# A graph-attention and low-rank expert kernel: the neighbours' sum as two float32r products of a split operand

## The chip, the cores and the metric

The kernel runs on one core of a Trainium2 chip. The metric is the device time of one execution in microseconds (us). The engines are named as in the profile: PE is TensorE (PEld its weight loads), DVE is VectorE, ACT is ScalarE, POOL is GpSimd and SP is SyncE, which here only issues transfers.

## The reference, cut to what matters

There are 128 images (batch entries) of 128 rows and 1024 columns, 16 heads of 64 columns, and 8 experts of rank 16.

```python
h  = layernorm(x)                              # x: (128, 128, 1024)
Wh = h @ W                                     # W: (1024, 1024), 16 heads of 64
e  = leaky_relu(Wh1 + Wh2, 0.2)                # one score per row and head
att = softmax(where(adj == 0, -9e15, e)) * adj # adj: 0/1, (128, 128, 128)
x  = x + elu(att @ Wh)
y  = layernorm(x)
gates = softmax(top2(y[:, 0, :] @ router_w.T)) # 2 of 8 experts for each image
x  = x + y + low-rank sum of the two chosen experts (y @ down, then @ up)
```

The score `e` depends on the row alone, not on the neighbour. So `att @ Wh` is one number per row and head times a plain sum of the neighbours' `Wh` with the 0/1 matrix `adj`. That product, "the neighbours' sum", is what the change rewrites.

## The kernel before, in words

**Tiling.** The images are handled in 64 pairs; `q` counts the pairs, images `2q` and `2q+1` are t = 0 and t = 1 of pair `q`. Two pairs make a group of four images, and the gates and experts are worked group by group (32 groups).

**Projection.** `project(q)` multiplies a pair by `W` with seven block products instead of eight (a Strassen-Winograd scheme on 2 x 2 blocks, the two images being one block dimension): `product_1`, `product_6`, `product_2`, `product_5`, `product_7`, `product_3`, `product_4`, in this order; below they are P1 to P7. Each is 8 matmuls of 260 columns in fp32 (L287). Their left operands are the transposed images `xt` and sums of them, which POOL makes in `pair_sums` (tiles `s1`, `s2`, `s4` and one in place). Results leave PSUM through ACT copies (L312, L316) and DVE additions (L299) into `u` tiles and the pair's tile `wh`. `wh[:, t, h]` has 512 columns of `Wh` and 8 score columns for image t and half h. `W` is centred over its rows beforehand, so `wh` lacks only the row scale 1/deviation, `rstd`, of the first layer norm.

**Attention.** `attention_weights(q)` first has ACT multiply the pair's two `adj_f` tiles by `rstd` (L361), since the neighbour's row scale belongs to the contracted index; then DVE makes the softmax factor `att` in small operations with one exponential on ACT (L371) between. `attend(i)` is the neighbours' sum of image i: two fp32 matmuls, one for each half, with `adj_f` as the stationary and `wh` as the moving operand (L389). `update(i)` multiplies by `att` (L399) and adds the ELU to `x` (L406 on ACT, L407 and L408 on DVE).

**Experts.** `second_stats` gives the second layer norm's scales. `turn(i)` transposes the updated image with a DMA (ACT copies to `halves`, L439, DMA to `tt`), and `rejoin` puts it into `y_t` (ACT, L445). `join` adds `y` to `x` in place (ACT, L461). For a group, `logits` makes the router's product (PE, L469), `choose` and `weigh` the two gates (DVE, with one exponential `pr` on ACT, L497), `fetch` spreads the choice over the partitions (PE `pb` L518, DVE `at_down` L520) and gathers the experts' rows with nine indirect DMAs on POOL's queue (`down` L532, `up` L536). `ffn_down` (PE `pd` L546, ACT `dn` L552) and `ffn_up` (PE `pu` L562, DVE L566) finish the group, and SP writes the result.

**Order of work.** All engine queues are in program order, written out by hand. In step q, eight lists of work `gaps[0]` to `gaps[7]` stand between the seven products: what is in `gaps[k]` is issued ahead of the (k+1)th product. `attention_weights(q-1)` is in gap 0, the two `attend` of pair q-1 in gaps 1 and 2. In odd steps `fetch` is at the head of gap 1, `ffn_down` of gap 4, and `ffn_up` in gaps 5 and 6. In even steps `logits`, `choose`, `weigh` are in gap 6, with `group_adj` and `load_adj` of another group behind them. So on PE an odd pair runs P1, `pb`, attend, P6, attend, P2, P5, `pd`, P7, `pu`, P3, `pu`, P4; an even one P1, attend, P6, attend, P2, P5, P7, P3, logits, P4.

**Buffers.** PSUM holds two tiles `pw` of two banks for the products and four one-bank tiles `pm` for all else. `xt`, `wh`, `hp`, `adj_f`, `tt`, `s1`, `s2`, `s4` have two buffers each, `x` ten.

Of the kernel before, what the change touches and what calls it, by code (L numbers as in the profile page):

```python
# [7 lines left out]

F32 = mybir.dt.float32
I32 = mybir.dt.int32  # L10
U32 = mybir.dt.uint32
U16 = mybir.dt.uint16
AF = mybir.ActivationFunctionType
ALU = mybir.AluOpType
# [9 lines left out]
def adj_ffn_kernel(  # L24
# [13 lines left out]
    nc = tc.nc  # L38
    B, N, D = x.shape
    P = 128  # L40
    KC = D // P
    KH = KC // 2
# [7 lines left out]
    HALF = 512  # L50
    NH = D // HALF
    HPH = HALF // F
    CPH = HALF // P
    NG, _, G, _ = adj.shape
    HE = HALF + HPH
# [3 lines left out]
    const = ctx.enter_context(tc.tile_pool(name="const", bufs=1))  # L59
    work = ctx.enter_context(tc.tile_pool(name="work", bufs=2))  # L60
# [6 lines left out]
        mybir.EngineType.PE, mybir.EngineType.DVE, mybir.EngineType.Activation,  # L67
        mybir.EngineType.Pool, mybir.EngineType.SP}))

    X, XT, MV, RSTD, WH, PH, SUMS, ATT, TT = ({} for _ in range(9))  # L70
    GRP = {}


# [6 lines left out]
    w_sb = const.tile([P, 7, KH, HE], F32, name="w_sb")  # L80
    BLOCK = [[B11, B21], [T1, B22]]

    def load_pair(q):
        XT[q] = work.tile([P, 2, KC, P], F32, tag="xt", name="xt")
        for t in range(2):
            nc.sync.dma_start(XT[q][:, t], x_t[2 * q + t])
        for i in (2 * q, 2 * q + 1):
            X[i] = work.tile([P, D], F32, tag="x", name="xn", bufs=10)
            nc.sync.dma_start(X[i], x[i])

    def load_adj(g):
        adj_i = work.tile([P, G, N], I32, tag="adj_i", name="adj_i", bufs=1)
        nc.sync.dma_start(adj_i, adj[g])
        adj_f = work.tile([P, G, N], F32, tag="adj_f", name="adj_f")
        nc.gpsimd.dma_start(adj_f, adj_t[g])
        GRP[g] = {"adj_i": adj_i, "adj_f": adj_f}

# [1 line left out]

        return w_sb[:, BLOCK[h][k // KH], k % KH]  # L100

    a_rows = work.tile([1, 2, D], F32, tag="wh", name="a_rows")
    nc.sync.dma_start(a_rows, a[None])
    for h in range(NH):
        for k in range(KC):
            (nc.scalar, nc.sync)[k % 2].dma_start(
                w_at(h, k)[:, 0:HALF], w[k * P:(k + 1) * P, h * HALF:(h + 1) * HALF])
    load_pair(0)
    router_sb = const.tile([P, KC, E], F32, name="router_sb")
    down_sb = work.tile([P, G * TOP, R, KC], F32, tag="down", name="down_sb", bufs=1)  # L110
    load_adj(0)
# [6 lines left out]
    nc.vector.memset(half_pow, -0.5)  # L118
    one_row = const.tile([1, P], F32, name="one_row")
    nc.vector.memset(one_row, 1.0)  # L120
    mean_of = const.tile([P, P], F32, name="mean_of")
    nc.vector.memset(mean_of, 1.0 / D)
    ones_g = const.tile([G, P], F32, name="ones_g")
    nc.vector.memset(ones_g, 1.0)
# [117 lines left out]
    def pair_sums(q):  # L242

        xt = XT[q]
        a11, a12 = xt[:, 0, 0:KH], xt[:, 0, KH:KC]
        a21, a22 = xt[:, 1, 0:KH], xt[:, 1, KH:KC]
        s1, s2, s4 = (work.tile([P, KH, P], F32, tag=n, name=n) for n in ("s1", "s2", "s4"))
        nc.gpsimd.tensor_tensor(s1, a21, a22, ALU.add)
        nc.gpsimd.tensor_tensor(s2, s1, a11, ALU.subtract)  # L249
        nc.gpsimd.tensor_tensor(a21, a11, a21, ALU.subtract)  # L250
        nc.gpsimd.tensor_tensor(s4, a12, s2, ALU.subtract)
        SUMS[q] = (s1, s2, a21, s4)

    def group_adj(g):

# [14 lines left out]
    def project(q):  # L270

        xt = XT.pop(q)
        a11, a12, a22 = xt[:, 0, 0:KH], xt[:, 0, KH:KC], xt[:, 1, KH:KC]
        s1, s2, s3, s4 = SUMS.pop(q)

        wh = WH[q] = work.tile([P, 2, NH, HE], F32, tag="wh", name="wh")

        def bank():
            return ps_w.tile([P, 2, HALF], F32, tag="pw", name="pw")

        def product(dst, first, lhs, rhs):
            for j in range(2):
                for k in range(KH):
                    nc.tensor.matmul(dst[:, j, 0:QE], lhs[:, k, :],  # L287
                                     w_sb[:, rhs, k, j * QE:(j + 1) * QE],
                                     start=(first and k == 0), stop=(k == KH - 1),
                                     skip_group_check=not first)  # L290

        def cols(t):
            return t.rearrange("p (j c) -> p j c", j=2)

        def temp(tag):
            return work.tile([P, HE], F32, tag=tag, name=tag, bufs=1)

        def read(dst, src, plus):
            nc.vector.tensor_tensor(cols(dst), src[:, :, 0:QE], cols(plus), ALU.add)  # L299

        p1, u2, u4 = (temp(n) for n in ("p1", "u2", "u4"))
        banks = {}

        def to(name):
            if name not in banks:
                banks[name] = bank()
                return banks[name], True
            return banks[name], False

        def product_1():  # L310
            product(*to("x"), a11, B11)
            nc.scalar.copy(cols(p1), banks["x"][:, :, 0:QE])  # L312

        def product_2():
            product(*to("x"), a12, B21)
            nc.scalar.copy(cols(wh[:, 0, 0]), banks["x"][:, :, 0:QE])  # L316

        def product_6():
            product(*to("y"), s2, T2)
            read(u2, banks["y"], p1)  # L320

        def product_5():
            product(*to("y"), s1, T1)
            read(u4, banks["y"], p1)
            if q == 0:
                read(wh[:, 1, 1], banks["z"], u4)

        def product_7():
            product(*to("z"), s3, T3)
            if q:  # L330
                read(wh[:, 1, 1], banks["z"], u4)

        def product_3():
            product(*to("y"), s4, B22)
            read(wh[:, 0, 1], banks["y"], p1)

        def product_4():
            product(*to("z"), a22, NT4)
            read(wh[:, 1, 0], banks["z"], u2)


        for step in ((product_1, product_6, product_2, product_5, product_7, product_3, product_4)
                     if q else
                     (product_1, product_2, product_6, product_7, product_5, product_3, product_4)):
            step()
            yield

    def attention_weights(q):

        g, first = divmod(2 * q, G)
        st = GRP[g]
# [2 lines left out]
        n1, n0, neg = (st[n][:, pair, None].to_broadcast(shape) for n in ("n1", "n0", "neg"))  # L356
        raw = WH[q].rearrange("p t h c -> p (t h) c")[:, :, HALF:HE]
        rstd = RSTD[q]
        for t in range(2):
            cols = st["adj_f"][:, first + t]  # L360
            nc.scalar.mul(cols, cols, rstd[:, t:t + 1])  # L361
        e = small.tile(shape, F32, tag="e", name="e")
        nc.vector.scalar_tensor_tensor(e.rearrange("p t (h c) -> p (t h) c", h=NH), raw, ALPHA,
                                       raw, op0=ALU.mult, op1=ALU.max)
# [4 lines left out]
        nc.vector.tensor_tensor(p[:, 0], e, m, ALU.subtract)  # L369
        nc.vector.tensor_tensor(p[:, 1], neg, m, ALU.subtract)  # L370
        nc.scalar.activation(p, p, AF.Exp)  # L371
        z = small.tile([P, 2, 2, H], F32, tag="z", name="z")
        nc.vector.tensor_mul(z[:, 0], p[:, 0], n1)
        nc.vector.tensor_mul(z[:, 1], p[:, 1], n0)
# [8 lines left out]
    def attend(i):  # L383

        g, t = divmod(i, G)
        wh = WH[i // 2][:, i % 2]
        PH[i] = [ps_m.tile([P, HALF], F32, tag="pm", name="ph") for _ in range(NH)]
        for h in range(NH):
            nc.tensor.matmul(PH[i][h], GRP[g]["adj_f"][:, t, :], wh[:, h, 0:HALF],  # L389
                             start=True, stop=True)  # L390

    def update(i):

# [190 lines left out]
    def prepare(gaps):  # L584

        prod = {}
        gaps[0] += [
            (spread_a,), (column_means, 0), (column_means, 1),
            (lambda: prod.update({1: score_products(1)}),),
            (score_columns_at_once, 0), (score_means, 0), (center_block, 0, B11),  # L590
            (pair_sums, 0), (weights_3_main,)]
        gaps[1] += [(center_block, 0, B21)]
        gaps[2] += [(lambda: score_columns(1, prod[1]),), (weights_3_scores,),
                    (combine, T2, T3, B11, ALU.add), (score_means, 1), (center_block, 1, T1)]
        gaps[3] += [(combine, T1, T1, B11, ALU.subtract)]
        gaps[4] += [(center_block, 1, B22)]
        gaps[5] += [(combine, NT4, B21, T2, ALU.subtract)]
        gaps[6] += [(first_stats, 0), (first_stats, 1)]

    NQ = B // 2  # L600


    for q in range(NQ + 2):
        gaps = [[] for _ in range(8)]
        if q == 0:
            prepare(gaps)
        g, part = divmod(q - 2, 2)
        ffn = 0 <= g < NG
        if ffn and not part:
# [15 lines left out]
            gaps[5] += [(join, i), (join, i + 1)]  # L625
        if q + 1 < NQ:
            gaps[3].append((first_stats, 2 * q + 2))
            gaps[4].append((pair_sums, q + 1))
            gaps[5].append((first_stats, 2 * q + 3))
        if ffn and part:  # L630
            gaps[1].insert(0, (fetch, g))
            gaps[4].insert(0, (ffn_down, g))
            gaps[5].insert(0, (ffn_up, (g, 0)))
            gaps[6].append((ffn_up, (g, 1)))
        if q % 2 == 0 and q < NQ:
            gaps[6].append((group_adj, q // 2))
            if q // 2 + 1 < NG:
                gaps[6].append((load_adj, q // 2 + 1))

        if q + 1 < NQ:  # L640
            load_pair(q + 1)
        if q == 1:
            slot, down_row, up_row = experts()
        products = project(q) if q < NQ else iter(())
# [41 lines left out]
```

## Time and profile before

| What | Value |
|---|---|
| Median of 3 runs | 2066.79 us (2066.38 to 2068.28) |
| The profiled execution's own time | 2068.33 us |
| Its span, first to last instruction | 2066.6 us |
| PE busy | 2022.0 us |
| DVE busy | 1526.5 us |
| ACT busy | 982.1 us |
| POOL busy | 835.3 us |
| Neighbours' sum on PE (L389), 512 records | 243.7 us busy |
| Mean granted TensorE clock | 0.987 |

All of it is one execution. A fp32 matmul appears as two records with a weight load each, so the 256 products of L389 are 512 records. Their busy times overlap a little; the time that a matmul adds is read from the distance of starts, or from the chain of work that ended last. In a timeline, the columns are the start, the duration in us, the engine, the line and operation, output and input, and in brackets the idle time of the engine ahead of it with what ended it. A bracket on an engine with nothing due later costs nothing.

### The profile page before, as it was taken

The numbers are of one execution on the slowest core, as the hardware profiler recorded it, in microseconds if no ns is written. First come the engines' busy times: TensorE is split into PE (matmuls) and PEld (weight loads), VectorE is DVE, ScalarE is ACT, GpSimd is POOL, SyncE is SP. The second block draws the span as 40 slices with busy tenths as digits, with TensorE's granted clock in tenths as the row PEclk, the third lists the DMA queues.
The fourth block names the chain that finished last, engine by engine and source line by source line (L and its number), as shares of the span: only waits on it lengthen the run. The fifth ranks groups of instructions, "written<-read, shape, count | busy, mean of one in ns | idle before, by whom it ended". The sixth has DMA issues, their size and how long they took to land.

```text
span 2066.6 us, 29670 instructions
## 1 busy us (share of the span) xinstructions
PE 2022.0 (98%) x10964; PEld 1571.0 (76%) x10964; DVE 1526.5 (74%) x3317; ACT 982.1 (48%) x899; POOL 835.3 (40%) x1041
## 2 busy tenths in 40 slices
PE   7999999999999999999999999999999999999994
PEld 4877777777777777777777777777777777777772
DVE  7778777778777778677778777777777777777774
ACT  0354454454454454454454454454454454454451
POOL 5243343443343443343443343443343443343431
PEclk9999999999999999999999999999999999999996
DMA  4346556555556555555555555545556545555632
GB/s 184 107 128 173 173 144 183 157 139 174 171 146 183 158 138 174 170 147 183 156 140 174 174 146 179 160 137 177 173 146 178 167 130 180 171 144 179 171 75 102
DMA packets 343170, 324.96 MB, mean 157 GB/s; under 512 B 274289, under 2 KB 275313, under 8 KB 343025
## 3 DMA queue, kind: packets, MB, share of 16 engines
q1 hardware_dynamic: 324178, 278.45, 46.2%
q0 software_dynamic: 17408, 41.96, 7.5%
q10 hardware_dynamic: 1440, 2.65, 0.4%
q8 instruction: 87, 1.43, 0.3%
q14 instruction: 57, 0.47, 0.1%
HBM read 189.31 MB, written 67.63 MB: 124 GB/s over the span
## 4 chain that ended last, share of the span: by engine, by line
PE 94%; DVE 3%; DMA 1%; POOL 1%; ACT 0%; issue 0%; ACTq 0%; POOLq 0%; DVEq 0%
PE pw L287 76%; PE ph L389 11%; PE pu L562 3%; PE pd L546 3%; PE pl L469 1%; POOL down L532 1%; PE pb L518 1%; DVE w_sb L194 0%; DVE prod L179 0%; DMA down<-table,at_down 0%; DMA w_sb<-in_w 0%; DMA tt<-halves 0%; DVE w_sb L180 0%; DVE hp L399 0%; DVE w_sb L173 0%
## 5 line engine op out<-in xcount | busy, mean ns | idle before, releaser
L287 PE MATMUL pw<-w_sb,xt 128*128 128x260 f32 x4096 | 942.5, 386 | 5.7 <-DVE w_sb L194 5.0
L287 PEld LDWEIGHTS pw<-w_sb,xt 128*128 128x128 f32 x4096 | 772.7, 190 | 178.0 <-issue 58.9
L287 PE MATMUL pw<-w_sb,s 128*128 128x260 f32 x3072 | 709.7, 384 | 4.3 <-DVE w_sb L582 3.5
L287 PEld LDWEIGHTS pw<-w_sb,s 128*128 128x128 f32 x3072 | 582.1, 190 | 143.3 <-issue 30.9
L532 POOL DMA_INDIRECT down<-table,at_down x256 | 291.1, 1137 | 339.1 <-DVE of_slot L526 260.9
L230 POOL TENSOR_SCALAR rstd<-mv 128x2 f32<-128x2 f32 x128 | 28.7, 224 | 826.6 <-DVE mv L227 825.4
L445 ACT COPY y_t<-tt 128x2048 uint16<-128x2048 uint16 x126 | 315.4, 2504 | 99.0 <-DMA tt<-halves 98.6
L226 DVE BATCH_NORM_STATS2 stats<-xn 128x6 f32<-128x512 f32 x512 | 324.7, 676 | 2.2
L299 DVE TENSOR_TENSOR wh<-pw,u 128x520 f32<-128x520 f32 x128 | 89.4, 698 | 274.5 <-PE pw L287 274.4
L439 ACT COPY halves<-xn 128x2048 uint16<-128x2048 uint16 x126 | 239.2, 1898 | 103.3 <-DVE xn L408 94.4
L406 ACT ACTIVATE ex<-hp 128x1024 f32<-128x1024 f32 x128 | 135.4, 1058 | 240.7 <-DVE hp L399 239.0
L389 PE MATMUL ph<-wh,adj_f 128*128 128x512 f32 x512 | 243.7, 598 | 0.0
L566 DVE SCALAR_TENSOR_TENSOR xn<-pu,rstd,xn 128x512 f32<-128x512 f32 x256 | 174.4, 744 | 29.8 <-PE pu L562 28.3
L399 DVE TENSOR_TENSOR hp<-ph,att 128x512 f32<-128x512 f32 x256 | 167.3, 675 | 38.0 <-PE ph L389 37.6
L408 DVE SCALAR_TENSOR_TENSOR xn<-ex,xn 128x1024 f32<-128x1024 f32 x128 | 156.8, 1225 | 14.1 <-DVE xn L407 0.5
L371 ACT ACTIVATE p<-p 128x64 f32<-128x64 f32 x64 | 16.4, 256 | 303.7 <-DVE p L370 303.7
L407 DVE SCALAR_TENSOR_TENSOR xn<-hp,xn 128x1024 f32<-128x1024 f32 x128 | 156.8, 1225 | 4.4
L461 ACT ACTIVATE xn<-xn,off,mul 128x1024 f32<-128x1024 f32 x128 | 151.3, 1231 | 0.8 <-POOL off L426 0.8
L389 PEld LDWEIGHTS ph<-wh,adj_f 128*128 128x128 f32 x512 | 94.7, 190 | 68.2 <-issue 50.0
L299 DVE TENSOR_TENSOR u<-pw,p 128x520 f32<-128x520 f32 x128 | 86.3, 674 | 17.6 <-PE pw L287 14.9
L231 POOL TENSOR_TENSOR rstd<-rstd,half_pow 128x2 f32<-128x2 f32 x128 | 91.8, 717 | 10.7
L249 POOL TENSOR_TENSOR s<-s,xt 128x512 f32<-128x512 f32 x64 | 81.7, 1277 | 5.0
(100 smaller groups left out, 1265.5 us busy)
## 6 DMA issues: line engine op xcount, KB each, us to landing
xt<-in_x_t SPq DMA_DIRECT2D x128, 512.0 KB
xn<-in_x SPq DMA_DIRECT2D x128, 512.0 KB
out_y<-xn SPq DMA_DIRECT2D x128, 512.0 KB
adj_f<-in_adj_t POOLq DMA_DIRECT2D x32, 256.0 KB
adj_i<-in_adj SPq DMA_DIRECT2D x32, 256.0 KB
down<-table,at_down POOLq DMA_INDIRECT x256
w_sb<-in_w ACTq DMA_DIRECT2D x8, 256.0 KB
w_sb<-in_w SPq DMA_DIRECT2D x8, 256.0 KB
```

Of the source, the lines that this page charges most:

```text
L226: nc.vector.bn_stats(st[:, h, :], X[i][:, h * HALF:(h + 1) * HALF])
L287: nc.tensor.matmul(dst[:, j, 0:QE], lhs[:, k, :], w_sb[:, rhs, k, j * QE:(j + 1) * QE], start=(first and k == 0), stop=(k == KH - 1), skip ...
L299: nc.vector.tensor_tensor(cols(dst), src[:, :, 0:QE], cols(plus), ALU.add)
L389: nc.tensor.matmul(PH[i][h], GRP[g]["adj_f"][:, t, :], wh[:, h, 0:HALF], start=True, stop=True)
L399: nc.vector.tensor_tensor(hp[:, h * HALF:(h + 1) * HALF].rearrange("p (h f) -> p h f", f=F), ph.rearrange("p (h f) -> p h f", f=F), att[:, ...
L407: nc.vector.scalar_tensor_tensor(xt, hp, 0.0, xt, op0=ALU.max, op1=ALU.add)
L408: nc.vector.scalar_tensor_tensor(xt, ex, 1.0, xt, op0=ALU.min, op1=ALU.add)
L439: nc.scalar.copy(halves, X[i].bitcast(U16).rearrange("p (d s) -> p s d", s=2))
L445: nc.scalar.copy(y_of(i).bitcast(U16).rearrange("p k (n s) -> p s k n", s=2), TT.pop(i).rearrange("p (s k) n -> p s k n", s=2))
L461: nc.scalar.activation(X[i], X[i], AF.Identity, bias=GRP[g]["off"][:, t:t + 1], scale=GRP[g]["mul"][:, t:t + 1])
L532: nc.gpsimd.indirect_dma_start(out=st["down"][:, j * R:(j + 1) * R].rearrange("p r k -> p (r k)"), out_offset=None, in_=table, in_offset=b ...
L566: nc.vector.scalar_tensor_tensor(y[:, cols], pu[t], st["rstd"][:, t:t + 1], y[:, cols], op0=ALU.mult, op1=ALU.add)
```

## The change

The row scale moves from `adj_f` to `Wh`. The scaled `Wh` is split into two float32r tiles: `high` (ACT) multiplies `wh` by `rstd` and rounds the result on writing to float32r, a 12-bit significand; `low` (DVE) takes the same product less the high part, also written as float32r. `attend` now makes two products for each half, `adj_f` by the high and by the low part, added up in PSUM. `adj_f` holds the plain 0 and 1 as float32r, and its scaling is gone. The new tile `parts` has one buffer; to make room, `wh`, `s1`, `s2` and `s4` go from two buffers to one, and `mean_of` shares a work buffer.

In the order of work: `high(t, h)` and `low(t, h)` for (0,0) come in gap 4, for (1,1) and (0,1) in gap 6, `high` for (1,0) in gap 7 and its `low` inside `attention_weights` of the next step, after the exponential is issued. On ACT in an even step this places two `high` behind the joins and ahead of `pr`; on DVE two `low` stand behind `group_adj`. The fourth of the pair sums becomes `last_sum` in gap 6. The second `first_stats` moves from gap 5 to 4, and for pair 0 both move to the start. The load of `x` is issued behind that of `xt`; for pair 0 it goes ahead of `w`.

```diff
-        adj_f = work.tile([P, G, N], F32, tag="adj_f", name="adj_f")
+        adj_f = work.tile([P, G, N], F32R, tag="adj_f", name="adj_f")
...
+    load_x(0)
     for h in range(NH):
         for k in range(KC):
             (nc.scalar, nc.sync)[k % 2].dma_start(
                 w_at(h, k)[:, 0:HALF], w[k * P:(k + 1) * P, h * HALF:(h + 1) * HALF])
-    load_pair(0)
+    load_xt(0)
...
-        s1, s2, s4 = (work.tile([P, KH, P], F32, tag=n, name=n) for n in ("s1", "s2", "s4"))
+        s1, s2 = (work.tile([P, KH, P], F32, tag=n, name=n, bufs=1) for n in ("s1", "s2"))
...
+    def last_sum(q):
+        s4 = work.tile([P, KH, P], F32, tag="s4", name="s4", bufs=1)
+        nc.gpsimd.tensor_tensor(s4, XT[q][:, 0, KH:KC], SUMS[q][1], ALU.subtract)
+        SUMS[q] += (s4,)
...
-        wh = WH[q] = work.tile([P, 2, NH, HE], F32, tag="wh", name="wh")
+        wh = WH[q] = work.tile([P, 2, NH, HE], F32, tag="wh", name="wh", bufs=1)
+        PARTS[q] = work.tile([P, 2, 2, NH, HALF], F32R, tag="parts", name="parts", bufs=1)
...
+    def high(q, t, h):
+        nc.scalar.mul(PARTS[q][:, 0, t, h], WH[q][:, t, h, 0:HALF], RSTD[q][:, t:t + 1])
+
+    def low(q, t, h):
+        nc.vector.scalar_tensor_tensor(PARTS[q][:, 1, t, h], WH[q][:, t, h, 0:HALF],
+                                       RSTD[q][:, t:t + 1], PARTS[q][:, 0, t, h].bitcast(F32),
+                                       op0=ALU.mult, op1=ALU.subtract)
+
     def attention_weights(q):
...
-        for t in range(2):
-            cols = st["adj_f"][:, first + t]
-            nc.scalar.mul(cols, cols, rstd[:, t:t + 1])
...
         nc.scalar.activation(p, p, AF.Exp)
+        low(q, 1, 0)
...
     def attend(i):
...
         for h in range(NH):
-            nc.tensor.matmul(PH[i][h], GRP[g]["adj_f"][:, t, :], wh[:, h, 0:HALF],
-                             start=True, stop=True)
+            for s in range(2):
+                nc.tensor.matmul(PH[i][h], GRP[g]["adj_f"][:, t, :], PARTS[q][:, s, i % 2, h],
+                                 start=(s == 0), stop=(s == 1))
...
+        if q < NQ:
+            gaps[4].append((high, q, 0, 0))
+            gaps[6] += [(high, q, 1, 1), (high, q, 0, 1)]
+            gaps[7].append((high, q, 1, 0))
...
         if q + 1 < NQ:
             gaps[3].append((first_stats, 2 * q + 2))
-            gaps[4].append((pair_sums, q + 1))
-            gaps[5].append((first_stats, 2 * q + 3))
+            gaps[4] += [(pair_sums, q + 1), (first_stats, 2 * q + 3)]
...
+        if q + 1 < NQ:
+            gaps[6].append((last_sum, q + 1))
...
+        if q < NQ:
+            gaps[4].append((low, q, 0, 0))
+            gaps[6] += [(low, q, 1, 1), (low, q, 0, 1)]
+
         if q + 1 < NQ:
-            load_pair(q + 1)
+            load_xt(q + 1)
+            load_x(q + 1)
```

## Prediction, made before the changed kernel was run

> **What bounds the kernel now.** I read the page first: the profiled execution took 2068.33 us for a span of 2066.6, and the median of the three runs is 2066.79, so I sum against 2068.33 and take 1.5 off at the end.
>
> ```profile
> PE 2022.0 (98%) x10964; PEld 1571.0 (76%) x10964; DVE 1526.5 (74%) x3317; ACT 982.1 (48%) x899; POOL 835.3 (40%) x1041
> ...
> PE 94%; DVE 3%; DMA 1%; POOL 1%; ACT 0%; issue 0%; ACTq 0%; POOLq 0%; DVEq 0%
> ...
> L389 PE MATMUL ph<-wh,adj_f 128*128 128x512 f32 x512 | 243.7, 598 | 0.0
> ```
>
> TensorE is never free, and the neighbours' sum (L389) is part of that. So less work there should pay, unless something else is almost as late. To see that I took one group of four images (two pairs) in the timelines: its period is 61.91 us, (1980.57 - 123.30) / 30 between equal places of the chain. The timeline of PE, 800 to 860 us:
>
> ```profile
> 822.43 3.67 PE L287 MATMUL pw<-w_sb,s 128*128 128x260 f32 x16
> 826.03 0.45 PE L546 MATMUL pd<-y_t,down 128*32 128x128 f32 x6
> 827.05 1.97 PE L546 MATMUL pd<-y_t,down 128*32 128x128 f32 x58 [0.58 <-DMA down<-table,at_down]
> ```
>
> Here the experts' product `pd` waits 0.58 us for the gathered rows `down`; in most groups it does not. The gather is thus as late as PE. What starts it, in the timelines of ACT, DVE and POOL (the last two lines are a group's first and last `down` issue):
>
> ```profile
> 992.63 0.29 ACT L497 ACTIVATE pr<-pr,lg 4x1 f32<-4x1 f32 x1 [0.65 <-DVE pr L496]
> ```
>
> ```profile
> 992.95 0.14 DVE L504 TENSOR_SCALAR val<-pr 4x1 f32<-4x1 f32 x1 [0.36 <-ACT pr L497]
> ...
> 998.89 0.23 DVE L520 TENSOR_SCALAR at_down<-pb,down_row 128x8 uint32<-128x8 f32 x1 [0.21 <-issue]
> ```
>
> ```profile
> 937.55 1.07 POOL L532 DMA_INDIRECT down<-table,at_down  x1 [8.51 <-DVE of_slot L526]
> ...
> 947.78 1.03 POOL L532 DMA_INDIRECT down<-table,at_down  x1 [0.30 <-issue]
> ```
>
> The gates `pr` come from ACT, DVE works in order to the row numbers `at_down`, and POOL issues eight gathers. In the tail PE starts at 2049.74 on rows issued at 2047.17, so a gather lands 2.57 us after its issue. From the end of `at_down` (937.27, same group as the POOL lines) to usable rows: 947.78 + 2.57 - 937.27 = 13.08 us.
>
> **The change, part by part.**
>
> *TensorE.* Four L389 records take 1.72 us in the chain, 0.86 for each fp32 product. Two single-pass products replace each. The trace has no such product: one fp32 record of 512 columns (0.43) bounds it above, and nothing but zero below; I take the middle, 0.215. An attend falls from 1.72 to 0.86, a group by 3.44, to 58.47 us of PE work. Alone that is 128 x 0.86 = 110 us.
> The Trainium skill (FP8 and Floating Point Precision, TensorE Precision Notes) gives true fp32 four passes; its page TensorE: Matmul & The Clock Gate (Back-to-back issue gap) gives one pass of 512 columns 216 ns, an estimate that no row here shows; by it the sum would be the same.
>
> *VectorE, four `low` per pair.* A two-input operation from SBUF takes 1.225 us at 1024 columns (L407) and 0.192 at 32 (L363): 0.69 at 512. In rows of four such operations (L566, 2.73) the later ones cost 0.66; L226 back to back costs 0.63. I take 0.64, bounds 0.63 and 1.04 (the start's L179 beside POOL). 256 x 0.64 = 164 us.
>
> *ScalarE, four `high` per pair* for two scalings of `adj_f`. Those two take 0.68; 1024 columns take 1.18 in a pair (L461), so 512 take about 0.70; two, overlapped, 1.36 (bounds 1.18, two COPY of L312, and 1.50, twice a point between L361 and L461 taken alone). ACT has the room (48%); its order matters: in an even pair `high` (1,1) and (0,1) now stand between the joins and `pr`.
>
> *The group's chain*, from one `pd` to the next, now that DVE and ACT carry more:
> - `pd`, two products, two `pu` on PE: 950.74 to 962.27, 11.53.
> - DVE: four adds 2.75; two `low` 1.28; then from the read of `wh` at 966.01 to the second image's last add, 980.62, 14.61 less the waits in it (0.32, 0.84, 0.17, 0.23) plus `low` (1,0), 13.69. Sum 17.72 (before: 18.35).
> - ACT `halves`, DMA transpose, `y_t`, joins: 980.62 to 991.98, 11.36. `high` (0,0) hides in the wait for the transpose.
> - Two `high` 1.36, `pr` to `val` 0.32 (before: 0.65 of waiting for `choose`, and 0.32).
> - DVE `val` to the end of `at_down`: 992.95 to 999.12, 6.17, less two waits (0.32, 0.21), plus three `low` 1.92: 7.56.
> - Gather 13.08.
>
> Sum 62.93; before, the same steps give 61.46, inside PE's 61.91. So the bound changes: +1.02 us a group, 31 groups, +31.6. PE idles 62.93 - 58.47 = 4.46 a group: some 0.35 at the logits, which wait for `y_t`, and 4.1 at `pd`; behind it stand P7, `pu`, P3 on PE, and `dn` and the odd `high` (0,0) on ACT, for which DVE's `low` waits. Uncertain: each 0.05 on `low` is 0.3 a group (six lie on the chain), gather 11.8 to 13.5.
>
> *The clock after such a stall.* PE's timeline near the start:
>
> ```profile
> 29.33 5.92 PE L287 MATMUL pw<-w_sb,xt 128*128 128x260 f32 x16 [4.97 <-DVE w_sb L194]
> 35.93 3.77 PE L287 MATMUL pw<-w_sb,xt 128*128 128x260 f32 x16 [0.68 <-ACT p L312]
> 43.24 5.46 PE L287 MATMUL pw<-w_sb,s 128*128 128x260 f32 x16 [3.53 <-DVE w_sb L582]
> 48.53 3.67 PE L287 MATMUL pw<-w_sb,xt 128*128 128x260 f32 x16
> ```
>
> After idle times of 3.53 and 4.97 us the same block takes 1.79 and 2.25 us longer, and the stretches of 1 us show the granted clock at 0.50 there; after 0.68 it does not. The clock changes at about 27.0, 33.7, 44.0 and 47.4, all multiples of 3.4 us apart; both drops end a stretch in which PE worked about 0.8 of 3.4 us. An idle time of 4.1 at a random place fills such a stretch about three times in four. Price 31 x 0.75 x 1.9 = 44 us (0 to 31 x 2.25 = 70); it lies on the chain, on `pd` and P7.
> This is the rule that speaks against the change: the Trainium skill (TensorE: Matmul & The Clock Gate, the HAM clock gate) halves the clock after an idle window of about 3.4 us, free-running; if only a wholly idle window counted, 4.1 us would do it one time in five, 12 us. The row after 3.53 is harsher.
>
> *Start.* `load_x(0)` goes ahead of `w` on SP: 1 MB at about 405 GB/s (the stretches from 20 us on) delays `w` by up to 2.6; `first_stats` moves to where DVE idles (3.8 to 12.6 us), leaving a busy stretch. 0 to 2.6, taken 1.3. *End:* `low` before the last weights, +0.6. *Edits at nothing:* on POOL `last_sum` now waits for P3, with the `adj_f` load and the gathers queued behind; those start over 10 us later, and `s4` is needed a pair later. `pair_sums` waits for P5, behind the gathers anyway. If that cover went, each is 1.28 a pair. Single buffers for `wh`, `parts`: their readers are done before P2 and P7 end. Swapping `xt` and `x` loads on SP, the same bytes, hides behind a pair of work; `adj_f` keeps its queue and size.
>
> Sum: 2068.3 + 31.6 + 44 + 1.3 + 0.6 = 2145.8; less 1.5 to the median: 2144.
>
> **Rivals.**
> 1. *Gather-bound, clock kept.* The idle is split (six `pd` records run early), so the clock stays: 2144 - 44 = 2100. Chance 0.20; the likeliest case, clock dropped, 0.53 (2110 to 2185).
> 2. *Not single-pass.* If a new product costs a whole record (0.43), attends stay 1.72, PE's idle falls to about 1.0, the chain is the same, the clock holds: 2100 again. Chance 0.06.
> 3. *Faster: the gather issues quicker.* In the tail, DVE idle, the eight issues span 8.95 us (2038.22 to 2047.17), not 10.23: 1.28 less. Against it: DVE is busier beside the gather, not idler. The period would be 61.65, 0.26 under before; the idle falls to 2.8, too short for most clock drops: 31 x 0.26 = 8 less, 1.9 more at start and end, 2061. It decides once the chain is 1.02 shorter than I sum; every further us is 31. Chance 0.13.
> 4. *Faster: PE stays the bound*, every wait hidden: 2068.3 - 110 + 1.9 - 1.5 = 1959. It needs the chain 4.5 shorter. Chance 0.04.
>
> The remaining 0.04 is no change.
>
> **How the numbers follow.** Slower 0.53 + 0.20 + 0.06 = 0.79, faster 0.17, same 0.04; 0.2% is about what a measurement of this kernel can tell from no change. The range takes cases 1, 2 and the likeliest, and the near part of 3: 2045 to 2185.
>
> **What would show it.** Right: PE waits of 3 to 5 us at `pd` for `down` in nearly every group; 5-us idle totals per group; granted clock under 0.95 on the mean; attend at 0.86; `pr` starting 1.4 us after the joins; period near 64.3. Wrong: `pd` without waits (then PE is the bound and rival 4 holds), waits with the clock at 1.0 (rival 1), or PE waiting elsewhere, for `parts` at the attends or for `u` at P5 of an odd pair, which has some 0.2 us of slack by these steps (a short wait there only comes off the one at `pd`).

## The result, and the profile after

| | before | after |
|---|---|---|
| Median, runs side by side | 2067.53 us (2066.38 to 2068.34, 4 runs) | 2081.09 us (2077.71 to 2085.27, 4 runs) |
| Ratio to before | | 1.0067, 95% interval 1.0048 to 1.0086 |
| Span of the profiled execution | 2066.6 us | 2079.3 us |
| Mean granted TensorE clock | 0.987 | 0.983 |

The change makes the kernel slower by 0.7%: 13.6 us, where 77 were forecast. The page of the kernel after, its busy times, its chain that ended last, and the groups of the changed operations:

```profile
PE 1957.9 (94%) x10964; PEld 1589.1 (76%) x10964; DVE 1735.0 (83%) x3573; ACT 1098.0 (53%) x1027; POOL 845.7 (41%) x1041
...
PE 35%; DVE 24%; DMA 13%; issue 11%; POOL 9%; ACT 6%; DVEq 0%; POOLq 0%; ACTq 0%
...
L360 ACT ACTIVATE parts<-wh,rstd 128x512 fp32r<-128x512 f32 x256 | 178.4, 715 | 287.3 <-DVE wh L308 287.1
...
L363 DVE SCALAR_TENSOR_TENSOR parts<-wh,rstd,parts 128x512 fp32r<-128x512 f32 x256 | 235.1, 939 | 29.6 <-ACT parts L360 29.5
...
L563 PE MATMUL pd<-y_t,down 128*32 128x128 f32 x2048 | 102.1, 306 | 81.6 <-DMA down<-table,at_down 81.6
...
L406 PE MATMUL ph<-parts,adj_f 128*128 128x512 f32 x512 | 161.8, 437 | 1.3 <-ACT parts L360 0.9
```

The chain that was 94% PE is now PE for only 35%; the rest is spread over DVE, the DMA, POOL and ACT: the loop through the group's work sets the time. PE waits for the gathered rows at `pd`, 81.6 us in the whole. PE's timeline for the `pd` of two neighbouring groups:

```profile
948.82 0.44 PE L563 MATMUL pd<-y_t,down 128*32 128x128 f32 x4
950.55 0.41 PE L563 MATMUL pd<-y_t,down 128*32 128x128 f32 x2 [1.29 <-DMA down<-table,at_down]
951.92 1.94 PE L563 MATMUL pd<-y_t,down 128*32 128x128 f32 x58 [0.96 <-DMA down<-table,at_down]
953.78 3.77 PE L296 MATMUL pw<-w_sb,xt 128*128 128x260 f32 x16
...
1010.57 0.44 PE L563 MATMUL pd<-y_t,down 128*32 128x128 f32 x4
1012.25 0.41 PE L563 MATMUL pd<-y_t,down 128*32 128x128 f32 x2 [1.23 <-DMA down<-table,at_down]
1013.71 2.89 PE L563 MATMUL pd<-y_t,down 128*32 128x128 f32 x58 [1.05 <-DMA down<-table,at_down]
1016.53 4.45 PE L296 MATMUL pw<-w_sb,xt 128*128 128x260 f32 x16
```

From the first `pd` record to P7 are 4.96 us, where an unhindered `pd` takes 1.91: the stall is 3.05 us, broken by six early records. Behind the second stall `pd` and P7 take 0.95 and 0.68 us longer, because the clock is down. The windows of 3.413 us around it (the column before the last two is the granted clock):

```profile
1007.68:1011.09 3.41, 3.34 (x18) 2.44 (x16) 3.27 (x4) 1.54 (x2) 2.68 (x3) 1.00 0.85 167
1011.09:1014.50 3.41, 1.20 (x31) 1.02 (x35) 3.24 (x8) 1.90 (x1) 2.90 (x5) 1.00 0.45 87
1014.50:1017.92 3.42, 3.42 (x41) 2.77 (x34) 1.98 (x5) 1.28 (x3) 3.25 (x6) 0.50 1.05 272
1017.92:1021.33 3.41, 3.41 (x18) 2.59 (x20) 1.87 (x2) 3.14 (x2) 2.25 (x3) 1.00 0.09 19
```

In ten of the 31 steady groups the clock is halved like this, each time for exactly one such window: 1.7 us of PE work lost. Without it the distance from one `pd` to the next is 61.77 us in the median of 21 periods (five of them are longer, 62.3 to 63.3), with it 63.31 in the median of nine.

The 12.7 us between the spans are then: +16.5 over the 30 periods from the first `pd` to the last steady one (139.92 to 2013.68 against 144.91 to 2002.18), -5.0 ahead of the first, +1.2 behind the last. Nine of the ten drops lie in those periods, and 9 x 1.7 are 15.3 of the 16.5; the rest of the period is as long as before. The tenth lies behind the last and is in the 1.2.

### The profile page after: what moved, and what is told of

Same layout as the page of the kernel before. It is cut to its first block, busy times and chain, and to the rows that moved or that the text cites. A ratio compares the mean times of both kernels' runs of the same rounds, so it can differ in the third digit from the quotient of the medians.

```text
span 2079.3 us, 29990 instructions
## 1 busy us (share of the span) xinstructions
PE 1957.9 (94%) x10964; PEld 1589.1 (76%) x10964; DVE 1735.0 (83%) x3573; ACT 1098.0 (53%) x1027; POOL 845.7 (41%) x1041
## 4 chain that ended last, share of the span: by engine, by line
PE 35%; DVE 24%; DMA 13%; issue 11%; POOL 9%; ACT 6%; DVEq 0%; POOLq 0%; ACTq 0%
PE pw L296 27%; POOL down L549 9%; DMA tt<-halves 7%; DMA down<-table,at_down 6%; ACT xn L478 4%; PE pd L563 4%; PE pu L579 3%; DVE parts L363 3%; DVE xn L425 2%; DVE hp L416 2%; DVE stats L230 2%; DVE xn L424 2%; ACT parts L360 2%; PE ph L406 1%; DVE u L308 1%
## 5 line engine op out<-in xcount | busy, mean ns | idle before, releaser
L549 POOL DMA_INDIRECT down<-table,at_down x256 | 271.7, 1061 | 372.1 <-DVE of_slot L543 293.1
L360 ACT ACTIVATE parts<-wh,rstd 128x512 fp32r<-128x512 f32 x256 | 178.4, 715 | 287.3 <-DVE wh L308 287.1
L363 DVE SCALAR_TENSOR_TENSOR parts<-wh,rstd,parts 128x512 fp32r<-128x512 f32 x256 | 235.1, 939 | 29.6 <-ACT parts L360 29.5
L563 PE MATMUL pd<-y_t,down 128*32 128x128 f32 x2048 | 102.1, 306 | 81.6 <-DMA down<-table,at_down 81.6
L416 DVE TENSOR_TENSOR hp<-ph,att 128x512 f32<-128x512 f32 x256 | 161.2, 671 | 3.8 <-issue 0.2
L406 PE MATMUL ph<-parts,adj_f 128*128 128x512 f32 x512 | 161.8, 437 | 1.3 <-ACT parts L360 0.9
L563 PEld LDWEIGHTS pd<-y_t,down 128*32 128x32 f32 x2048 | 77.3, 146 | 107.1 <-issue 78.6
L259 POOL TENSOR_TENSOR s<-xt,s 128x512 f32<-128x512 f32 x64 | 81.5, 1274 | 136.4 <-PE pw L296 136.4
```

Source lines behind the costliest of these rows:

```text
L360: nc.scalar.mul(PARTS[q][:, 0, t, h], WH[q][:, t, h, 0:HALF], RSTD[q][:, t:t + 1])
L363: nc.vector.scalar_tensor_tensor(PARTS[q][:, 1, t, h], WH[q][:, t, h, 0:HALF], RSTD[q][:, t:t + 1], PARTS[q][:, 0, t, h].bitcast(F32), op0 ...
L416: nc.vector.tensor_tensor(hp[:, h * HALF:(h + 1) * HALF].rearrange("p (h f) -> p h f", f=F), ph.rearrange("p (h f) -> p h f", f=F), att[:, ...
L549: nc.gpsimd.indirect_dma_start(out=st["down"][:, j * R:(j + 1) * R].rearrange("p r k -> p (r k)"), out_offset=None, in_=table, in_offset=b ...
L563: nc.tensor.matmul(pd[t * GR:(t + 1) * GR, 0:P], st["down"][:, t * GR:(t + 1) * GR, k], st["y_t"][:, k, t * P:(t + 1) * P], start=(k == 0) ...
```

## The experiments

Chain theory: the loop `pd`, DVE, transposes, gates, gather sets the period, the drops of the clock come on top. Its rivals: PE is still the bound, or DVE or ACT by its total. The kernels of a part ran on one chip; each ratio is to the kernel before there, whose median was 2066.2 to 2067.9 us on all of them, so that times of different parts can be set side by side to a microsecond or two. They change the kernel after, unless their name says before.

### Is it the chain?

**pr_first.** The two `high` of gap 6 go behind `pr` on ACT.

```diff
-            gaps[6] += [(high, q, 1, 1), (high, q, 0, 1)]
...
             gaps[6] += [(logits, g), (choose, g), (weigh, g)]
+        if q < NQ:
+            gaps[6] += [(high, q, 1, 1), (high, q, 0, 1)]
```

> The changed kernel with the gates' exponential ahead of the two high operations on ACT (in the even step). Chain theory (each group is set by the run gates, row numbers, gather, experts' product, at 61.7 us a group, with 3.0 us of PE idle at pd): val moves from 993.42 to about 992.72, the chain loses 0.7 us a group, the stall falls to 2.3; 31 x 0.7 = 22 less, and some of the ten clock drops (1.6 each) go: 2050 to 2060. VectorE-bound theory (its added 164 us are simply too much): same work in the same order on DVE, no change, 2081. PE-bound theory: no change, 2081.

Measured: 2043.73 us, ratio 0.9888 (0.9871 to 0.9904). The period falls to about 61.0 and only two drops of the clock are left. Putting two ACT operations, 1.2 us of work, behind `pr` gains 37 us, more than was expected.

**fetch_early.** The gather's indices are worked out one gap earlier.

```diff
-            gaps[1].insert(0, (fetch, g))
+            gaps[0].insert(0, (fetch, g))
```

> The changed kernel with fetch (pb, at_down and the gather) at the head of gap 0, so DVE makes the row numbers before, not after, the softmax factors of that step. Chain theory: at_down 3.1 us earlier, the stall at pd closes, PE waits some 0.3 for own at pb; period 59.0 instead of 62.5 on the mean, no clock drops: 2079 - 31 x 3.45, about 1974, mean clock 0.99. VectorE-bound theory: DVE has the same work, 2081. PE-bound theory: 2081.

Measured: 2025.08 us, 0.9788 (0.9768 to 0.9808): faster, but 51 us short of the expectation. The last issue on POOL and `pd` on PE, in their timelines:

```profile
984.46 0.94 POOL L549 DMA_INDIRECT down<-table,at_down  x1 [0.30 <-issue]
```

```profile
987.29 0.45 PE L563 MATMUL pd<-y_t,down 128*32 128x128 f32 x6
988.87 1.93 PE L563 MATMUL pd<-y_t,down 128*32 128x128 f32 x58 [1.12 <-DMA down<-table,at_down]
```

Issued earlier, the rows land 4.4 us after the last issue; in the kernel after it is 2.7 (1011.01 to 1013.71). What runs behind that last issue is the transpose of an image, issued by SP at 984.04. The transpose in SP's timeline, and three windows with the DMA engines' share in the column before the last:

```profile
984.04 7.25 SPq L458 DMA_TRANSPOSE tt<-halves  x2
```

```profile
977.00:981.00 4.00, 4.00 (x20) 3.42 (x19) 3.66 (x8) 1.06 (x1) 3.08 (x4) 1.00 0.73 283
981.00:985.00 4.00, 4.00 (x20) 3.47 (x19) 3.97 (x7) 1.90 (x1) 3.08 (x4) 1.00 0.17 48
985.00:988.00 3.00, 2.75 (x17) 1.93 (x15) 2.83 (x4) 1.64 (x3) 2.05 (x2) 1.00 0.99 201
```

The loads of the next pair have faded by 981. The transpose's packets run from 985.26 to 988.20 in the trace, the gather's queue moves nothing from 985.32 to 987.75, and `pd` starts at 988.87. It is so in all 31 steady groups: `pd` starts 0.55 to 1.03 us behind the transpose's last packet. In the kernel after the transpose comes earlier against the issues (1008.61 to 1011.58, the last issue at 1011.01), and it is the rows of the two issues before that wait. By these times the gather waits behind the transpose; no run moved the transpose by itself.

**attend_twice.** Each of the four products is issued twice.

```diff
-            for s in range(2):
+            for s in range(4):
-                nc.tensor.matmul(PH[i][h], GRP[g]["adj_f"][:, t, :], PARTS[q][:, s, i % 2, h],
-                                 start=(s == 0), stop=(s == 1))
+                nc.tensor.matmul(PH[i][h], GRP[g]["adj_f"][:, t, :], PARTS[q][:, s % 2, i % 2, h],
+                                 start=(s % 2 == 0), stop=(s % 2 == 1))
```

> The changed kernel with each of the four products of an attend issued twice (the second set overwrites the first): PE gets 0.86 to 0.94 us more for each image, 3.4 to 3.8 a group, nothing else changes. Chain theory: the added work fills the stall of 3.0; period 61.8 to 62.5, no clock drops: 2065 to 2085, not slower. PE-bound theory: 128 x 0.86 = 110 more, 2190.

Measured: 2101.51 us, 1.0168 (1.0151 to 1.0185). PE got 0.92 us more in every attend, some 118 us in all, and the time rose by 20: the rest went into the stall and the drops of the clock. The waits at `pd` of this kernel:

```profile
PE pd L563 <- DMA down<-table,at_down: 16.1, 14, 4.5
```

They were 81.6 us in 66 waits. No drop of the clock is left in the steady groups, and PE is the bound again, at 62.85 us a group in the median. That is above the range expected (2065 to 2085): 3.68 us of added work a group are more than the stall of 3.05 could take.

**chain_longer.** Three more `low` ahead of `at_down` on DVE.

```diff
+        for _ in range(3):
+            if 2 * g + 2 < NQ:
+                low(2 * g + 2, 1, 0)
```

> The changed kernel with low (1,0) issued three more times (the same values) just ahead of at_down, in the odd steps only: 1.98 us of DVE work on the chain of each group. Chain theory: period up by 1.98, stall at pd 5.0 us, longer than a clock stretch of 3.4, so the clock drops in nearly every group instead of one in three, 1.6 us each: 31 x (1.98 + 1.05) = 94 more, 2175, mean clock 0.95 to 0.97; if the clock drops do not depend on the stall's length, 61 more, 2142, clock 0.983. VectorE-bound theory: 61 more, 2142. PE-bound theory: 2081.

Measured: 2179.44 us, 1.0552 (1.0535 to 1.057); mean clock 0.959. Two microseconds more on the chain cost 98 in all, since the clock now drops in all 31 steady groups, in seven of them for two windows (the stall is 5.25 us in the median). Both parts of the chain theory hold; PE's and DVE's totals do not explain +4.7% against after.

### What was the chain in the kernel before?

**before_one_pass.** PE alone is relieved in the kernel before.

```diff
-        adj_f = work.tile([P, G, N], F32, tag="adj_f", name="adj_f")
+        adj_f = work.tile([P, G, N], F32R, tag="adj_f", name="adj_f")
...
-        wh = WH[q] = work.tile([P, 2, NH, HE], F32, tag="wh", name="wh")
+        wh = WH[q] = work.tile([P, 2, NH, HE], F32R, tag="wh", name="wh")
```

> The kernel before with one edit: adj_f (still scaled by rstd) and wh are written as float32r, so that the neighbours' sum is one single-pass product for each half. It leaves out the low part, so its numbers are those of 12-bit operands. Nothing of the change's DVE, ACT or order of work is in it; PE alone is relieved, by about 1.27 us an attend, 5.1 a group (to 56.8). Chain theory (the group's chain by way of the gather stood just behind PE in the kernel before as well): by the steps as measured (gather 12.6, joins' part 11.0) that chain is 60.6 to 61.0 a group; the period falls only to that, PE waits about 4 us at pd, and the clock drops in a third to three quarters of the groups: 2040 to 2060. PE theory (PE alone bounded the kernel before, and what the change lost is DVE's and ACT's new work): 2066 - 128 x 1.27 = 1904.

Measured: 1975.33 us, 0.9557 (0.9541 to 0.9573). Neither theory's number. PE waits at `pd` here too:

```profile
1020.93 0.44 PE L547 MATMUL pd<-y_t,down 128*32 128x128 f32 x4
1021.60 0.41 PE L547 MATMUL pd<-y_t,down 128*32 128x128 f32 x2 [0.23 <-DMA down<-table,at_down]
1022.48 1.97 PE L547 MATMUL pd<-y_t,down 128*32 128x128 f32 x58 [0.47 <-DMA down<-table,at_down]
```

So the chain is the bound, at 59.0 us in the group shown (58.7 in the median group): 2.45 less than the prediction had summed for the kernel before, and there is no drop of the clock with stalls this short (1.4 us in the median group). Step by step, in us (a group from 963.47 to 1022.48 here, from 951.92 to 1013.71 in after):

| Step | before, as predicted | before_one_pass | after, as predicted | after |
|---|---|---|---|---|
| `pd` to the first add behind the second `pu` | 11.53 | 11.50 | 11.53 | 11.50 |
| DVE to the second image's last add | 18.35 | 17.13 | 17.72 | 17.56 |
| transpose, `y_t`, joins | 11.36 | 11.29 | 11.36 | 10.91 |
| two `high`; wait for `choose`; `pr` to `val` | 0.97 | 0.32 | 1.68 | 1.53 |
| `val` to the end of `at_down` | 6.17 | 6.17 | 7.56 | 7.69 |
| gather | 13.08 | 12.60 | 13.08 | 12.60 |
| sum | 61.46 | 59.01 | 62.93 | 61.79 |

In the kernel before, DVE waited for PE and `pr` for `choose`, and the eight gather issues spanned 10.22 us (median of the groups) instead of 9.60 (why the issues are slower there was not settled). The two waits were slack, not length. Against 59.0 the change's new work adds 2.8 us a group, and the chain had not 0.4 but 2.8 us to give (61.85 less 59.0).

**before_fetch_early.** The edit of fetch_early on the kernel before.

> A control: the kernel before with fetch at the head of gap 0 instead of gap 1, the same edit as in fetch_early. If PE is the bound there with the chain by way of the gather just behind it, an earlier gather buys nothing but the few waits at pd (0.58 us in the group shown, none in most): 2060 to 2067. If the gather decided already, it would gain as it did on the changed kernel, 2.0 to 2.7%: 2010 to 2025.

Measured: 2065.7 us, 0.9992 (0.9982 to 1.0001). An earlier gather buys nothing where PE is the bound: its distance between `pd` is 61.85 with no waits. The gain of fetch_early belongs to the changed kernel's chain.

**adj_between.** fetch_early, and `group_adj` goes between `choose` and `weigh` on DVE, where DVE waits for `pr`:

```diff
-            gaps[6] += [(logits, g), (choose, g), (weigh, g)]
+            gaps[6] += [(logits, g), (choose, g)]
+        if q % 2 == 0 and q < NQ:
+            gaps[6].append((group_adj, q // 2))
+        if ffn and not part:
+            gaps[6].append((weigh, g))
```

> fetch_early, and in an even step DVE's group_adj is moved from behind weigh to between choose and weigh, where DVE waits for pr anyway (1.05 us idle in the trace of after). Chain theory: at_down comes up to 1.0 us earlier, the wait at pd (1.1 shown) goes nearly away, the period falls from 60.25 by 0.8 to 1.0: 1993 to 2003. If DVE's total work is what bounds (it is 83% busy), or the transfers that run beside the gather are, moving work between waits gives nothing: 2020 to 2030.

Measured: 1986.43 us (1985.45 to 1988.18), 0.9607 (0.9591 to 0.9623). Faster than both kernels of the case, and a little faster than expected. PE's timeline has no wait at `pd`:

```profile
1071.71 0.38 PE L296 MATMUL pw<-w_sb,xt 128*128 128x260 f32 x1
1072.55 0.39 PE L535 MATMUL pb<-own,ones_g 4*128 4x16 f32 x2 [0.46 <-DVE own L526]
1072.87 3.77 PE L296 MATMUL pw<-w_sb,xt 128*128 128x260 f32 x16
1076.29 1.28 PE L406 MATMUL ph<-parts,adj_f 128*128 128x512 f32 x4
1077.40 3.67 PE L296 MATMUL pw<-w_sb,s 128*128 128x260 f32 x16
...
1088.94 1.99 PE L563 MATMUL pd<-y_t,down 128*32 128x128 f32 x64
```

The period is 59.22: PE's own work of 58.76 and 0.46 at `pb`, which in this order waits for `own`.

**low_behind.** adj_between, and in even steps the two `low` of gap 6 go behind `fetch`, into the next step:

```diff
+            if q % 2:
+                gaps[0] += [(low, q - 1, 1, 1), (low, q - 1, 0, 1)]
...
-            gaps[6] += [(low, q, 1, 1), (low, q, 0, 1)]
+            if q % 2:
+                gaps[6] += [(low, q, 1, 1), (low, q, 0, 1)]
```

> adj_between, and in even steps the lows (1,1) and (0,1) are moved from gap 6 (ahead of val and at_down on DVE) to gap 0 of the next step, behind fetch. The chain loses another 1.3 us. Chain theory: no wait is left at pd, PE becomes the bound at its own work of about 58.9 a group: about 1970 to 1985; the rest of the difference to rival 4 (1959) is what the four-product attend costs over 0.86. If the lows now come too late for the attends (needed in gaps 1 and 2), PE waits there instead and the time stays at that of adj_between.

Measured: 1985.27 us, 0.9599 (0.9583 to 0.9615), the same as adj_between, with the same period of 59.22. With PE as the bound already, a shorter chain gains nothing.

### The new work by itself, and the start

**high_only.** `low` and its product are left out.

```diff
-        low(q, 1, 0)
...
-            for s in range(2):
+            for s in range(1):
...
-            gaps[4].append((low, q, 0, 0))
-            gaps[6] += [(low, q, 1, 1), (low, q, 0, 1)]
```

> The changed kernel without low and without its product (one product for each half; it leaves out the low part of Wh). ScalarE's highs, the order of work and the new start stay. before_one_pass showed that the chain by way of the gather, without highs and lows, is 59.0 a group; after showed 61.8. If that difference is the new work itself, the highs ahead of pr are 0.84 of it (1.22 for two, less 0.38 in the joins) and the lows the other 1.95: this kernel's chain is 59.85, PE waits at pd some 2 us, the clock drops in a few groups: 1998 to 2012. If the lows only fill DVE's waits and the highs or the new order hold the gather up, it stays at 2060 to 2080.

Measured: 2039.22 us, 0.9873 (0.9848 to 0.9897), some 30 us over the expectation. Where the clock holds, the period is 59.6 to 60.2, 59.85 in the median, as expected. But the clock is halved 19 times (once for two windows), and mostly in one group after another: the drops begin at 316.20, 377.64, 439.08 and 500.52, 61.44 us apart, which is 18 windows of 3.413. Windows of its trace ahead of and in two drops, and of a group without one:

```profile
435.66:439.08 3.42, 1.62 (x10) 0.79 (x8) 3.35 (x6) 1.92 (x2) 2.70 (x5) 1.00 0.55 115
439.08:442.49 3.41, 3.29 (x58) 3.13 (x58) 2.44 (x6) 0.00 (x0) 3.16 (x6) 0.50 0.94 230
...
497.10:500.52 3.42, 1.69 (x11) 0.84 (x9) 3.35 (x6) 1.96 (x2) 2.72 (x4) 1.00 0.56 119
500.52:503.93 3.41, 3.37 (x58) 3.14 (x58) 2.48 (x6) 0.00 (x0) 3.13 (x6) 0.50 0.95 213
558.54:561.95 3.41, 1.88 (x12) 1.00 (x10) 3.34 (x6) 2.17 (x2) 2.77 (x4) 1.00 0.65 128
561.95:565.37 3.42, 2.73 (x62) 2.47 (x63) 2.70 (x6) 0.73 (x2) 3.08 (x7) 1.00 0.86 195
```

A window in which PE works 1.62 or 1.69 us halves the next; 1.88 us does not. A drop lengthens the period from 59.8 to about 61.5, nearly 18 windows, so the next stall falls on the same place of the grid and drops again.

**start_alone.** The change's new start (the load of `x` ahead of `w`, both `first_stats` in gap 0, `xt` ahead of `x`) on the kernel before.

```diff
+    load_x(0)
...
-    load_pair(0)
+    load_xt(0)
...
-            (spread_a,), (column_means, 0),
+            (spread_a,), (first_stats, 0), (first_stats, 1), (column_means, 0),
...
-        gaps[6] += [(first_stats, 0), (first_stats, 1)]
...
-            load_pair(q + 1)
+            load_xt(q + 1)
+            load_x(q + 1)
```

> The kernel before with the change's new start alone: the load of x ahead of w for pair 0, both first_stats in DVE's idle time at the start, xt ahead of x in the loads. By the prediction's term +1.3 us (0 to 2.6): 2067 to 2070. By the trace of after, in which the second pair's first product begins 2.8 us earlier than before, -2.8: 2063 to 2065. The order of the xt and x loads was put at nothing.

Measured: 2066.26 us, 0.9993 (0.9984 to 1.0002). The second pair's first product starts at 66.58 instead of 69.09, but only some 1 us of that is left at the end, and the interval holds zero. The forecast's +1.3 lies outside that interval (-3.3 to +0.4 us).

### Is it the clock?

**fill_stall** and **high_only_fill.** Ten useless products just ahead of `pd`, in the kernel after and in high_only.

```diff
+    def fill(i):
+        g, t = divmod(i, G)
+        spare = ps_m.tile([P, HALF], F32, tag="pm", name="spare")
+        for _ in range(10):
+            nc.tensor.matmul(spare, GRP[g]["adj_f"][:, t, :], PARTS[i // 2][:, 0, i % 2, 0],
+                             start=True, stop=True)
...
             gaps[4].insert(0, (ffn_down, g))
+            if q <= NQ:
+                gaps[4].insert(0, (fill, 2 * q - 1))
```

> The changed kernel with useless work added on PE in every group: ten more single-pass products into a spare PSUM bank, right ahead of pd, 2.2 us of PE in which it would wait for the gather anyway. The chain by way of the gather is not touched; the stall of about 3 us shrinks to under 1. In the trace of after the clock was halved in nine of the groups, for 3.41 us each (about 1.7 us of PE work lost). If those drops come of the stall, as the prediction's clock term has it, and cost what they seem to, the added work makes the kernel faster: 2081 - 9 x 1.7 = 2066 (2062 to 2069), without a drop in the steady groups. If the drops cost nothing on the chain, or have another cause, the time stays at 2078 to 2085, or rises with the added work.

> The same ten products ahead of pd in high_only. There the clock was halved 19 times in the steady groups, at distances that are multiples of 61.44 us = 18 x 3.413, though its stall is shorter than that of after. If the miss of high_only against its expectation (2039 for 1998 to 2012) is the clock and not the chain, this kernel has the chain's own period, 59.85, and no drops: 2036 - 19 x 1.7 + 3 = 2007 (1999 to 2010). If the chain was mis-sized instead, it stays at 2034 to 2047.

Measured: 2065.53 us for fill_stall, 0.999 (0.9981 to 1.0), and 2005.71 for high_only_fill, 0.9706 (0.969 to 0.9722). No steady group has a drop in either. PE's timeline of fill_stall:

```profile
942.37 2.67 PE L413 MATMUL spare<-parts,adj_f 128*128 128x512 f32 x10
944.97 0.45 PE L570 MATMUL pd<-y_t,down 128*32 128x128 f32 x6
945.90 1.94 PE L570 MATMUL pd<-y_t,down 128*32 128x128 f32 x58 [0.49 <-DMA down<-table,at_down]
947.77 3.77 PE L296 MATMUL pw<-w_sb,xt 128*128 128x260 f32 x16
```

Added work that fills the stall makes the kernels faster, by 15.6 and 33.5 us; ten and twenty windows of 1.7 would be 17 and 34. So the drops are a cost on the path that sets the end, they come of PE's idleness, and the whole of the change's loss is here: the kernel after without them takes as long as the kernel before.

## Why the prediction was right in its direction and wrong in its size

**The mechanism was right.** The relief of PE uncovers the loop through the gather; PE waits at `pd` in every group; a clock loss comes on top; slower. attend_twice, chain_longer and the two filled kernels show each part. Two terms of the sum failed, by about 30 us each: the clock and the chain. That the direction held rests on the drops of the clock alone.

**The clock term failed by 28 us**: "fills such a stretch about three times in four", 31 x 0.75 x 1.9 = 44 us (the prediction's own numbers, 4.1 us idle and at most 0.8 of 3.4 worked, give two times in three). Measured: ten of 31, 15.6 us in all (fill_stall). The price of one drop was near; the share was not. The stall was 3.05 us and in pieces, not 4.1 whole, and its place on the grid is not random: with a period of 61.7 us, 18.08 windows, it moves by 0.3 us a group, and a drop moves it half a window away. The line that was taken, 0.8 us of work in a stretch, was wrong the other way: windows with up to 1.8 us of work are followed by a drop, and the stalls of 5.25 us in chain_longer bring one in every group. Rival 1's outcome, the clock kept, came in 21 groups of 31; whether because the stall is split, as it says, was not tried.

**The chain's sum failed by as much**: it was 1.14 us too long, 62.93 for 61.79, so that +31.6 us became about zero. The terms were the gather (13.08, measured 12.60), the transposes and joins (11.36 for 10.91), the two `high` (1.36 for 1.22) and DVE's part (17.72 for 17.56). The largest, the gather, came from an execution paced by PE; the joins' part was read from one group, while the median of the same trace is 10.98. A quicker gather is rival 3's case, "the gather issues quicker": its condition, a chain 1.02 us shorter, was met, and with the drops filled the time is 2065.5 against its 2061. The drops that remain are what the rival left out.

**The chain before was 2.45 us too long by the prediction's steps**: 61.46, 0.4 us inside PE's period, where before_one_pass shows 59.0. Its sums thus make the new work 1.47 us a group, where 2.8 were measured. The forecast set only the changed chain against PE's 61.91, so this didn't enter the time; but it hid that the change uses up 2.8 us of slack. Nothing in the prediction foresaw that the chain and PE's old period come out level, 61.8 and 61.85.

**Smaller terms.** A product costs 0.23 us (attend_twice: 0.92 for four) where 0.215 was taken; an attend is 1.12 from start to start, and the product ahead of it leaves 0.19 earlier, so 0.93 net where 0.86 was summed. Rival 2 falls by this. The Trainium skill's page TensorE: Matmul & The Clock Gate (Back-to-back issue gap) gives 216 ns for one pass of 512 columns, without naming float32r; the 0.23 here is near it. `low` takes 0.66 to 0.75 us on the chain (0.64 taken); the (0,0) one, beside POOL's pair sums, takes 1.59, above the bound of 1.04, and costs nothing there. Start: -5.0 ahead of the first `pd` for +1.3; start_alone has its first `pd` 2.45 us earlier than before (142.46 for 144.91), the rest was not taken apart. End: +1.2 for +0.6, a drop included.

**Rival 4** (PE stays the bound, 1959) is what adj_between reached by moving two pieces of DVE's work, at 1986: the rest is mostly 0.46 us a group at `pb` and 0.07 more in each of the four attends.

**The signs set out beforehand.** Right: PE's waits for `down` in every group (3.05 us, at the low end), `pr` 1.2 us behind the joins. Wrong: mean clock under 0.95 (it is 0.983), a period near 64.3 (62.46 on average), an attend at 0.86 (0.93) and 5 us of idle time a group (61.77 less PE's own 58.76 are 3.0).

## What to carry to other kernels

When one engine is the bound, the lengths read along any other loop hold that engine's slack: relieve the engine in a throwaway kernel (fewer passes for its products) and read the loop there, before costing a change that relieves it. New work on other engines must be put where they wait already, or behind what starts the critical transfer: here the same operations in another order took 95 us off the changed kernel. And a TensorE stall that leaves a clock window about half empty can cost more than its length, so a filler that keeps the engine busy can be worth its while until the stall itself is gone.

## What was not expected of the hardware

The clock's windows lie on a fixed grid of 3.413 us through the whole execution: in high_only the 19 drops begin at times that agree to 0.01 us modulo 3.4133. By these runs a drop goes with how little PE works in the window ahead of it, and the line is near one half. Over five kernels (after, pr_first, fetch_early, chain_longer, high_only), the 64 windows at full clock ahead of a drop in steady groups show PE busy 0.12 to 0.53 of the window; the lowest without a drop behind them are 0.46, 0.46, 0.49, 0.49 and 0.50, and before_one_pass has one of 0.43. Where the window is itself at half clock the line lies higher: of the eight that are followed by a second one (chain_longer, high_only) seven show PE busy 0.73 to 0.78 and one 0.45; the lowest that are not are 0.74 and 0.77. The Trainium skill (TensorE: Matmul & The Clock Gate, The HAM clock gate) has the free-running window of 3413 ns, as measured here, and says that the half rate comes after an idle window; by these runs the window need not be idle, only about half empty. Busy time is not quite what is counted: at the start of the kernel before, a window that the profile shows wholly busy (64.43 to 67.84 us, the narrow products of the router and the experts' centring) has a drop behind it too.

The number of drops does not follow the length of the stall alone. The stall of high_only is shorter than that of after (medians 2.6 and 3.0 us in the groups with a full clock), but its slowed period is nearly a multiple of the grid, and it drops 19 times against ten.
